# A decoder kernel: in both cross-attentions Pool subtracts the maximum, the scores are transposed, then the exponential leaves PSUM

## The chip, the cores and the metric

The kernel runs on one core of one Trainium2 chip. The metric is device time in microseconds (us) of one execution. The core has five engines, which run their own instruction streams in order and wait for each other by semaphores: TensorE (PE in the profile; PEld is its weight load), VectorE (DVE), ScalarE (ACT), GpSimd (POOL) and SyncE (SP), which here issues every DMA. SBUF holds 128 partitions of working memory; matrix products land in PSUM, of which the kernel uses eight banks of 128 x 512 float32.

## The reference

Two decoder layers over x of shape (8, 256, 256): eight batches, 256 tokens, width 256, all float32. Every sublayer is followed by a residual sum and a layer norm (post-norm):

```
x = LN(x + gated_recurrence(x))                       # layer 0
x = LN(x + cross_attention(x, ctx, bias, mask))       # 16 heads of 16
x = LN(x + ternary_ffn(x))                            # needs max|x| over ALL batches
x = LN(x + self_attention(x))                         # layer 1, relative positions
x = LN(x + cross_attention(x, ctx, mask))
x = LN(x + gated_ffn(x))                              # hidden 768
```

The attention that matters here is, for a head h,

```
scores = (q_h @ k_h.T) / 4 + bias       # 256 x 256; masked keys get -inf
attn   = softmax(scores, axis=keys)
out_h  = attn @ v_h                     # 256 x 16
```

There are 8 x 16 heads in each of three attentions: 128 in the first cross-attention, 128 in the self-attention, 128 in the second cross-attention.

## The kernel before

**An order worked out in advance.** The kernel doesn't loop over stages. Every batch of every sublayer is a Python generator that yields operations (`do(engine, cost, ready, emit)`), DMAs, buffer requests (`get`) and events. A planner (`Order.run`) keeps a clock for each engine, takes the operation that can start first, settles near-ties by an urgency number, and emits its instructions. Costs are written in by hand. The result is a fixed instruction stream for each engine, so what the chip does late the later instructions of that engine wait for. `place(x, n)` gives urgencies: the items stand in a row, the eight first cross-attentions at 0 to 7, then self-attentions and second cross-attentions interleaved by `S1_AT` and `X1_AT`, then feed-forwards by `F1_AT`. `loads()` has urgency 0, so all weight loads come before the first context load in SP's queue. Filler tasks (`keys_values`: the second cross-attention's keys and values, kept in DRAM) take what is left.

**Stages.** Recurrences of all batches come first, then the eight first cross-attentions with the last recurrences between them. A barrier follows (the ternary feed-forward needs the largest value of all batches), then the ternary feed-forward, then self-attention. Self-attention sends its relative-position scores and its probabilities through DRAM scratch (`sk`, `pb`), to shift each row by its position. From the third self-attention on, second cross-attentions run between; when all self-attentions are done, gated feed-forwards join.

**An attention item** (`ai` 0, 1, 2 for first cross, self, second cross; `it.whole` is true for the two cross-attentions) projects q, k and v, then goes through four quads n = 0 to 3, each of four heads j. `quad` (L897) computes the scores of four heads into four PSUM banks (`s`, L914). For each head DVE then adds bias or mask, negates, writes the result to SBUF (`sn`, one of four `s_bufs`) and finds the row's minimum `nm`, that is minus the maximum (L942, two instructions of 128x256, each followed by an accumulator read). `head` (L952) lets ACT take exp(nm - sn) into a slice of `p` (a tile of four heads; three of them), with the row sum as accumulator (L958, two instructions and two accumulator reads). PE transposes the head's 256 x 256 in four 128 x 128 pieces into PSUM (`pt`, L503), and ACT or DVE, whichever the planner finds earlier, copies it to SBUF (`pts`, L291/L292; eight buffers). `values` (L983) multiplies by v: head j of a quad lands in partitions 32j to 32j+31 of the item's PV bank. The two heads i = 0, 1 that share these partitions are told apart by v, which is 32 columns wide with zeros beside the 16 values, so both add into one result.

`scales` (L1019) turns the sums into reciprocals on DVE (`rsum`), POOL spreads them over 256 columns (`rsw`, L1028), PE transposes them (`ps_rs`), a copy brings them to `oT`. `attend_out` (L1041) multiplies PV by `oT` on DVE (L1050), projects (`pso`, L520), adds the residual (`xb`, L1058 on POOL, L1070 on DVE) and normalises. At most two items hold a PV bank at a time (`pv_left`).

**Buffers that are shared.** `p` (3), `s` (4), `v` (2), `q` (3), `k` (2) and `y` (2) serve all three attentions. The query and key weights arrive padded (32 columns a head of which 16 are used, 512 KB a matrix, `wpad`) in a `p` tile, and POOL compacts them (`compact`, L477).

## Time and profile before

Three runs took 817.53, 820.76 and 822.42 us; the median is 820.76.

| what | value |
|---|---|
| median of the runs | 820.76 us |
| span of the profiled execution (first to last instruction) | 807.4 us |
| the profiled execution's own time | not listed; the three runs stand 10.1, 13.4 and 15.0 us above this span |
| instructions | 21273 |
| DMA | 77.67 MB, mean 96 GB/s, 177681 packets, 155046 of them under 512 B |
| granted PE clock, mean | 0.998 |

In the page's groups a line is: source line, engine, operation, output <- input tiles, shape, count | busy us, mean ns of one | idle time of the engine just before, and what ended it. A busy share is an average over stages with different limits, so the stretches are read one by one. Matmuls are pipelined: a record of one includes its latency, and a busy PE is not a PE at its peak. A float32 matmul leaves two records, a transpose one. The profile lists the busy time of weight loads separately from matmuls because the two overlap.

### The profile page before, as it was taken

Reading aid. Unit: us, or ns where it says so; the run is one execution under the profiler, and the core shown is the slowest. Engines: PE = TensorE matmul, PEld = TensorE weight load, DVE = VectorE, ACT = ScalarE, POOL = GpSimd, SP = SyncE. Lnnn points to the kernel's source line nnn. Section 1 sums busy time; section 2 is a strip of 40 time slices with the busy share of each in tenths; the row PEclk is TensorE's granted clock in tenths of the full one; section 3 lists DMA queues with packets and bytes.
Section 4 is the critical chain, followed back from the end, with each engine's and each line's share of the span. In section 5 each row is a group of like instructions: output and inputs, shape, how many; then the busy total and the mean of one; then the engine's idle time right before and its main releaser. Section 6 shows DMA issues by size and latency. Waiting matters only on the chain. (4 is left out here: it accounts for less than half of the span.)

```text
span 807.4 us, 21273 instructions
## 1 busy us (share of the span) xinstructions
PE 774.9 (96%) x7175; PEld 597.3 (74%) x7175; DVE 703.4 (87%) x2461; ACT 629.7 (78%) x2036; POOL 210.4 (26%) x398
## 2 busy tenths in 40 slices
PE   7999999999999999997999999999999999999995
PEld 6787777777766787665767677767776767899885
DVE  3998989989787698887799999898898999989986
ACT  2339999899988457786597799999999899845942
POOL 4440321122111044233333304313242323110010
PEclk9999999999999999999999999999999999999999
DMA  5736352100100449889978706743656333100001
GB/s 183 221 120 97 26 74 50 40 15 28 40 14 15 144 116 220 173 166 154 192 159 170 137 7 145 166 87 89 121 120 139 85 72 114 40 15 16 26 14 39
DMA packets 177681, 77.67 MB, mean 96 GB/s; under 512 B 155046, under 2 KB 171430, under 8 KB 177574
## 3 DMA queue, kind: packets, MB, share of 16 engines
q1 hardware_dynamic: 177574, 76.32, 43.4%
q8 instruction: 57, 0.93, 0.5%
q14 instruction: 50, 0.41, 0.2%
HBM read 41.66 MB, written 34.64 MB: 94 GB/s over the span
## 5 line engine op out<-in xcount | busy, mean ns | idle before, releaser
L958 ACT ACTIVATE p<-sn,nm 128x256 f32<-128x256 f32 x768 | 381.5, 510 | 14.1 <-DVE nm L942 8.2
L503 PE MATMUL pt<-ident,p 128*128 128x128 f32 x1536 | 208.4, 278 | 4.3 <-ACT p L958 1.8
L503 PEld LDWEIGHTS pt<-ident,p 128*128 128x128 f32 x1536 | 169.4, 141 | 50.5 <-ACT p L958 30.2
L292 ACT COPY pts<-pt 128x512 f32<-128x512 f32 x277 | 148.3, 591 | 34.5 <-PE pt L503 29.6
L958 ACT ACTIVATION_READ_ACCUMULATOR p<-sn,nm 128x1 f32 x768 | 154.4, 201 | 0.0
L914 PE MATMUL s<-k,q 32*128 32x256 f32 (+2 forms) x1792 | 118.6, 370 | 0.5 <-ACT pts L292 0.3
L998 PE MATMUL pv<-pts,v 128*32 128x256 f32 x1536 | 104.0, 385 | 0.0
L942 DVE CUSTOM_DVE_ANT_0 sn<-s,bias 128x256 f32<-128x256 f32 x256 | 93.1, 419 | 10.0 <-ACT p L958 5.8
L942 DVE CUSTOM_DVE_ANT_0 sn<-s,hide 128x256 f32<-128x256 f32 x256 | 92.8, 418 | 8.2 <-PE s L914 5.3
L942 DVE CUSTOM_DVE_ANT_0 sn<-s,band 128x256 f32<-128x256 f32 x256 | 92.3, 418 | 8.6 <-PE s L914 3.5
L914 PEld LDWEIGHTS s<-k,q 32*128 32x128 f32 x1792 | 77.2, 185 | 30.1 <-issue 20.1
L291 DVE COPY pts<-pt 128x512 f32<-128x512 f32 x107 | 71.1, 683 | 6.7 <-PE pt L503 6.3
L998 PEld LDWEIGHTS pv<-pts,v 128*32 128x32 f32 x1536 | 41.7, 109 | 41.5 <-issue 19.1
L942 DVE DVE_READ_ACCUMULATOR2_ANT nm<- 128x1 f32 x768 | 63.0, 82 | 0.0
L1028 POOL COPY rsw<-rsum 128x512 f32<-128x512 f32 x24 | 14.6, 610 | 157.4 <-DVE rsum L1022 139.0
L520 PE MATMUL pso<-wvo,oT 128*128 128x256 f32 x192 | 46.3, 385 | 0.4 <-ACT pts L292 0.4
L520 PEld LDWEIGHTS pso<-wvo,oT 128*128 128x128 f32 x192 | 35.1, 190 | 7.8 <-issue 1.3
L1354 POOL COPY band<-ends 64x256 f32<-64x256 f32 x64 | 21.5, 360 | 70.8 <-DVE nm L942 70.8
L1426 DVE TENSOR_REDUCE acc<-tail 128x8 f32<-128x864 f32 x32 | 33.4, 1045 | 5.3 <-POOL tail L1415 5.3
L1327 POOL COPY w<-w 128x504 f32<-128x504 f32 x32 | 19.6, 613 | 68.8 <-DVE w L291 40.7
L1709 ACT ACTIVATE sg<-fg 128x512 f32<-128x512 f32 x24 | 14.3, 599 | 21.7 <-PE fg L1698 21.6
L520 PE MATMUL psv<-wvo,ctxT 128*128 128x256 f32 x128 | 30.8, 384 | 0.0
(197 smaller groups left out, 1321.3 us busy)
## 6 DMA issues: line engine op xcount, KB each, us to landing
sk<-w SPq DMA_DIRECT2D x32, 416.0 KB
band<-sk SPq DMA_DIRECT2D x64, 104.0 KB
pb<-p SPq DMA_DIRECT2D x64, 104.0 KB
band<-sk SPq DMA_DIRECT2D x64, 84.0 KB
pb<-p SPq DMA_DIRECT2D x64, 84.0 KB
acc<-pb SPq DMA_DIRECT2D x32, 156.0 KB
ctxT<-in_ctxT SPq DMA_DIRECT2D x16, 256.0 KB
wpad<-in_qk_w SPq DMA_DIRECT2D x6, 512.0 KB
```

The lines of the kernel that those rows point to most:

```text
L291: ("DVE", on_dve(n), lambda: nc.vector.tensor_copy(dst, src)),
L292: ("ACT", on_act(n), lambda: nc.scalar.copy(dst, src)),
L503: nc.tensor.transpose(ps[:, c, t * P : (t + 1) * P], src[:, t, c * P : (c + 1) * P], ident)
L520: nc.tensor.matmul(ps[:, t, :], srcT[:, c, t * P : (t + 1) * P], w[:, c, :], start=(c == 0), stop=(c == KC - 1),)
L914: nc.tensor.matmul(ps[j].tile[:, t, first : first + w], it.q.tile[32 * j : 32 * j + 32, c, t * P : (t + 1) * P], k[32 * j : 32 * j + 32, c ...
L942: nc.vector.tensor_tensor_reduce(out=s.tile[:, t, :], in0=ps[j].tile[:, t, :], in1=tile[:, t, :], scale=-1.0, scalar=3e38, op0=ALU.add, op ...
L958: nc.scalar.activation(p.tile[:, j, q, :], s.tile[:, q, :], AF.Exp, bias=nm[:, q : q + 1], scale=-1.0, accum_out=it.sum_of(q, h),)
L998: nc.tensor.matmul(it.pv.tile[32 * j : 32 * j + 32, c, :], it.v.tile[:, k, head_of(n, j), :], pts.tile[:, k, :], start=(k == 0 and i == 0 ...
L1028: lambda: nc.gpsimd.tensor_copy(wide.tile.rearrange("p t (h d) -> p t h d", d=DH), rs.unsqueeze(3).to_broadcast([P, NQ, H, DH]),),
L1327: nc.gpsimd.tensor_copy(w.tile[:, :, NR:], w.tile[:, :, NR - 1 : NR].to_broadcast([P, HH, PBW - NR]))
L1354: nc.gpsimd.tensor_copy(band.tile[0:BLK, :, t, lo:hi], it.ends[c][0:BLK, t, i:HH:2].unsqueeze(2).to_broadcast([BLK, 4, hi - lo]),)
L1426: lambda: nc.vector.tensor_reduce(acc[:, c, :, own, 1], tail.tile, AX.X, ALU.add),
```

## The change

In the two cross-attentions (`whole`), the work of a head is reordered:

- DVE writes negated scores and their row minimum as before. POOL then subtracts the minimum in place (two instructions of 128x256). PE transposes the scores, not the probabilities. ACT takes the exponential while moving the result from PSUM to `pts`, in one instruction of 128x512, without accumulators. No choice between ACT and DVE is left at this point.
- The row sums come from the value product. v is still 32 columns wide, but the 16 columns beside the values hold ones, so a head's 32 partitions of PV hold 16 values and 16 copies of the sum. Heads i = 0 and 1 can no longer add into one result. The quads are taken in the order (c, i) = (0,0), (1,0), (0,1), (1,1); after two quads DVE transposes the PV bank in 32x32 blocks to an SBUF tile `u`, and the next two quads start the bank anew. The third value product therefore waits for that transpose. `divided` then takes reciprocals of the sums, multiplies, and after the second half transposes back into `oT`. `scales` and the multiplication in `attend_out` remain for self-attention alone.
- Scores of the first cross-attention lie in twelve slices of the three `p` tiles, those of the second in the four `s` tiles. Self-attention writes its scores straight into `p` and takes the exponential in place.
- `v` is split: two tiles with ones (the second cross-attention uses one of them), and two zeroed tiles for self-attention. `y` and `u` have two tiles in layer 0 and one in layer 1.
- The transposes ask for their bank and their `pts` tile together, for all three attentions; the planner learns to treat operations that need two kinds of buffers, and to drop its reservations (`patient`) when it would otherwise be stuck.
- Query and key weights are loaded without padding, in two DMAs a matrix of 128 KB each, in runs of 64 bytes; `compact` is gone.
- The first cross-attention's mask is loaded into the tile that holds its float form; the second one's float mask becomes bfloat16.

The diff, cut to its core and moved left by one step:

```diff
-            if needs:
-                slots = needs[0].slots
-                if id(slots) in kept:
-                    continue
-                if len(slots.idle) < len(needs):
-                    if ready <= self.clock + 0.5:
+            short = False
+            for slots in {id(x.slots): x.slots for x in needs}.values():
+                count = sum(x.slots is slots for x in needs)
+                if id(slots) in kept or len(slots.idle) < count:
+                    short = True
+                    if patient and ready <= self.clock + 0.5:
                         kept.add(id(slots))
...
                 slots.idle.sort()
-                ready = max(ready, slots.idle[len(needs) - 1][0])
+                ready = max(ready, slots.idle[count - 1][0])
+            if short:
+                continue
             for engine, cost, emit in ways:
...
 pv_left = Slots(2, None)
-p_bufs = slots(work, "p", 3, [P, 4, NQ, S])
+ps_tiles = [work.tile([P, 4, NQ, S], F32, name=f"p{i}") for i in range(3)]
+p_bufs = kept(ps_tiles)
+early_bufs = kept([t[:, j] for t in ps_tiles for j in range(4)])
 pts_bufs = slots(work, "pts", 8, [P, NQ, S])
-s_bufs = slots(work, "s", 4, [P, NQ, S])
+late_bufs = slots(work, "s", 4, [P, NQ, S])
+u_tiles = [work.tile([P, NB, 3, DH], F32, name="u0"), w0.tile([P, NB, 3, DH], F32, name="u1")]
 q_bufs = slots(work, "q", 3, [P, KC, S])
...
 oT_bufs = slots(work, "oT", 2, [P, KC, S])
-y_bufs = slots(work, "y", 2, [P, NQ, D])
+y_tiles = [work.tile([P, NQ, D], F32, name="y0"), w0.tile([P, NQ, D], F32, name="y1")]
 xb_bufs = slots(work, "xb", 2, [P, NQ, D])
...
-v32s = []
-for i in range(2):
-    t = const.tile([P, NQ, H, 32], F32, name=f"v32_{i}")
-    nc.gpsimd.memset(t, 0.0)
-    v32s.append(t)
-v_bufs = kept(v32s)
+v_tiles = [pool.tile([P, NQ, H, 32], F32, name=f"v{i}") for i, pool in enumerate((const, w0))]
+for t in v_tiles:
+    nc.gpsimd.memset(t, 1.0)
+class Layer:
+    def __init__(self, n, s_bufs):
+        self.s_bufs = s_bufs
+        self.y_bufs, self.u_bufs, self.v_bufs = (kept(x[:n]) for x in (y_tiles, u_tiles, v_tiles))
+layers = [Layer(2, early_bufs), Layer(1, late_bufs)]
...
                 )
-            packed = yield from get(p_bufs, f"wpad{o}")
-            t = packed.tile.rearrange("p k c s -> p (k c s)")[:, 0 : KC * H * 32]
-            t = t.rearrange("p (c o) -> p c o", c=KC)
-            w = pool.tile([P, KC, D], F32, tag=f"wqk{o}", name=f"wqk{o}")
-            ready = yield from dma(
-                [packed.at], 524288,
-                lambda: nc.sync.dma_start(
-                    out=t, in_=chunked(qk_w[o])
-                ),
-            )
-            order.spawn(50 + o, compact(o, packed, t, w, ready))
+            w = wqk[o] = pool.tile([P, KC, D], F32, tag=f"wqk{o}", name=f"wqk{o}")
+            for c in range(KC):
+                events["wqk", o] = yield from dma(
+                    [0.0], 131072,
+                    lambda: nc.sync.dma_start(
+                        out=w[:, c, :].rearrange("p (h d) -> p h d", d=DH),
+                        in_=qk_w[o][c * P : (c + 1) * P, :].rearrange(
+                            "p (h w) -> p h w", w=32
+                        )[:, :, 0:DH],
+                    ),
+                    60,
+                )
             wvo[o] = pool.tile([P, KC, D], F32, tag=f"wvo{o}", name=f"wvo{o}")
...
         return (what, self.ai, self.b, *more)
+def parts_of(it, n):
+    if it.whole:
+        return n % 2, n // 2
+    return n // 2, n % 2
+def value_columns(it, v):
+    if it.whole:
+        return v.rearrange("p (h w) -> p h w", w=32)[:, :, 0:DH]
+    return bass.AP(
+        tensor=v.tensor, offset=v.offset, ap=[list(v.ap[0]), [64, H // 2], [48, 2], [1, DH]],
+    )
...
         order.spawn(urgency(it, n + 1, -12), quad(it, n + 1, parts, bias))
-    p = yield from get(p_bufs, f"p{it.name}_{n}", t_s)
+    p = None
+    if not it.whole:
+        p = yield from get(p_bufs, f"p{it.name}_{n}", t_s)
     left = [4]
...
     for j in range(4):
-        s = yield from get(s_bufs, f"sn{it.name}_{n}_{j}", t_s)
+        if it.whole:
+            s = yield from get(it.layer.s_bufs, f"sn{it.name}_{n}_{j}", t_s)
+            dst, t_dst = s.tile, s.at
+        else:
+            dst, t_dst = p.tile[:, j], p.at
         nm = small.tile([P, NQ], F32, tag="nm", name=f"nm{it.name}_{n}_{j}")
...
                 nc.vector.tensor_tensor_reduce(
-                    out=s.tile[:, t, :], in0=ps[j].tile[:, t, :], in1=tile[:, t, :], scale=-1.0,
+                    out=dst[:, t, :], in0=ps[j].tile[:, t, :], in1=tile[:, t, :], scale=-1.0,
                     scalar=3e38, op0=ALU.add, op1=ALU.min, accum_out=nm[:, t : t + 1],
                 )
-        t = yield from do("DVE", 0.7, [t_s, t_b, t_bias, s.at], emit)
+        t = yield from do("DVE", 0.7, [t_s, t_b, t_bias, t_dst], emit)
         ps[j].drop(t)
-        order.spawn(urgency(it, n), head(it, n, j, p, s, nm, t, left, times))
+        if it.whole:
+            order.spawn(urgency(it, n), head_whole(it, n, j, s, nm, t))
+        else:
+            order.spawn(urgency(it, n), head(it, n, j, p, nm, t, left, times))
     if it.ai == 1:
         it.bands[n].drop(t)
-def head(it, n, j, p, s, nm, t, left, times):
-    h = head_of(n, j)
+def head_whole(it, n, j, s, nm, t):
+    def emit():
+        for q in range(NQ):
+            nc.gpsimd.tensor_scalar(
+                s.tile[:, q, :], s.tile[:, q, :], nm[:, q : q + 1], None, ALU.subtract
+            )
+    t = yield from do("POOL", 0.66, [t], emit)
+    ps = Held(banks, f"pt{it.name}_{n}_{j}")
+    pts = Held(pts_bufs, f"pts{it.name}_{n}_{j}")
+    t = yield from do("PE", TURNS, [t, ps, pts], lambda: transposed(ps.tile, s.tile))
+    s.drop(t)
+    t = yield from do(
+        "ACT", on_act(512), [t, pts.at],
+        lambda: nc.scalar.activation(pts.tile, ps.tile, AF.Exp, scale=-1.0),
+    )
+    ps.drop(t)
+    it.turned[n].append((j, pts, t))
+    if len(it.turned[n]) == 4:
+        order.spawn(urgency(it, n), values(it, n))
+def head(it, n, j, p, nm, t, left, times):
+    h = head_of(*parts_of(it, n), j)
     def emit():
...
             nc.scalar.activation(
-                p.tile[:, j, q, :], s.tile[:, q, :], AF.Exp, bias=nm[:, q : q + 1], scale=-1.0,
+                p.tile[:, j, q, :], p.tile[:, j, q, :], AF.Exp, bias=nm[:, q : q + 1], scale=-1.0,
                 accum_out=it.sum_of(q, h),
             )
-    t_e = yield from do("ACT", 1.0, [t, p.at], emit)
-    s.drop(t_e)
+    t_e = yield from do("ACT", 1.0, [t], emit)
     it.t_sums.append(t_e)
...
     times.append(t_e)
-    if it.ai == 1 and len(times) == 4:
+    if len(times) == 4:
         it.tails(n, p, left, max(times))
     ps = Held(banks, f"pt{it.name}_{n}_{j}")
-    t = yield from do("PE", TURNS, [t_e, ps], lambda: transposed(ps.tile, p.tile[:, j]))
+    pts = Held(pts_bufs, f"pts{it.name}_{n}_{j}")
+    t = yield from do("PE", TURNS, [t_e, ps, pts], lambda: transposed(ps.tile, p.tile[:, j]))
     left[0] -= 1
...
         p.drop(t)
-    pts = yield from get(pts_bufs, f"pts{it.name}_{n}_{j}", t)
     t = yield from copy([t, pts.at], pts.tile, ps.tile)
...
 def values(it, n):
-    c, i = divmod(n, 2)
+    c, i = parts_of(it, n)
     t_v = yield from event(it.key("v"))
...
         it.pv = Held(banks, f"pv{it.name}")
+    if it.whole and n == 2:
+        t_turned = yield from event(it.key("turned", 0))
+        t_v = max(t_v, t_turned)
     parts = sorted(it.turned[n], key=lambda x: x[0])
...
                     it.pv.tile[32 * j : 32 * j + 32, c, :],
-                    it.v.tile[:, k, head_of(n, j), :],
+                    it.v.tile[:, k, head_of(c, i, j), :],
                     pts.tile[:, k, :],
-                    start=(k == 0 and i == 0 and (it.whole or c == 0)),
-                    stop=(k == NQ - 1 and i == 1 and it.whole),
+                    start=(k == 0 and (it.whole or n == 0)),
+                    stop=(k == NQ - 1 and it.whole),
                     tile_position=(0, 32 * j),
...
         it.v.drop(t)
+    if it.whole and n % 2 == 1:
+        order.spawn(urgency(it, n), divided(it, n // 2, t))
+    elif n == NS - 1:
         order.spawn(urgency(it, NS), attend_out(it, t))
     events[it.key("values", n)] = t
+def divided(it, i, t):
+    if i == 0:
+        it.u = yield from get(it.layer.u_bufs, f"u{it.name}", t)
+        it.rec = small.tile([P, 2, NB], F32, tag="rec", bufs=4, name=f"rec{it.name}")
+    u = it.u.tile
+    t = yield from do(
+        "DVE", on_dve(512), [t, it.u.at],
+        lambda: nc.vector.transpose(
+            u[:, :, i : i + 2, :].rearrange("p n a d -> p n (a d)"),
+            it.pv.tile.rearrange("p c (n e) -> p (c n) e", e=32),
+        ),
+    )
+    events[it.key("turned", i)] = t
+    if i == 1:
+        it.pv.drop(t)
+        it.token.drop(t)
+    def emit():
+        nc.vector.reciprocal(it.rec[:, i, :], u[:, :, i + 1, 0])
+        nc.vector.tensor_tensor(
+            u[:, :, i, :], u[:, :, i, :],
+            it.rec[:, i, :].unsqueeze(2).to_broadcast([P, NB, DH]), ALU.mult,
+        )
+    t = yield from do("DVE", 0.6, [t], emit)
+    if i == 0:
+        return
+    it.oT = yield from get(oT_bufs, f"oT{it.name}", t)
+    t = yield from do(
+        "DVE", on_dve(512), [t, it.oT.at],
+        lambda: nc.vector.transpose(
+            it.oT.tile.rearrange("p c (n e) -> p (c n) e", e=32),
+            u[:, :, 0:2, :].rearrange("p n a d -> p n (a d)"),
+        ),
+    )
+    it.u.drop(t)
+    order.spawn(urgency(it, NS), attend_out(it, t))
...
     ai, b = it.ai, it.b
-    t = yield from event(it.key("scales"))
+    t = t_pv
+    if ai == 1:
+        t = yield from event(it.key("scales"))
+        t_pv = yield from event(it.key("distances"))
+        t = yield from do(
+            "DVE", on_dve(512), [t, t_pv],
+            lambda: nc.vector.tensor_tensor(it.oT.tile, it.pv.tile, it.oT.tile, ALU.mult),
+        )
+        it.pv.drop(t)
+        it.token.drop(t)
     oT = it.oT
-    if ai == 1:
-        t_pv = yield from event(it.key("distances"))
-    t = yield from do(
-        "DVE", on_dve(512), [t, t_pv],
-        lambda: nc.vector.tensor_tensor(oT.tile, it.pv.tile, oT.tile, ALU.mult),
-    )
-    it.pv.drop(t)
-    it.token.drop(t)
     xb = yield from get(xb_bufs, f"xb{it.name}", t)
...
     t_b = yield from dma([bias.at], 262144, lambda: nc.sync.dma_start(out=bias.tile, in_=tokens(bias_in[b])))
-    mask = yield from get(mask_bufs, f"mask{b}")
-    t_m = yield from dma([mask.at], 262144, lambda: nc.sync.dma_start(out=mask.tile, in_=tokens(mask0_in[b])))
+    neg = yield from get(neg_bufs, f"neg{b}")
+    mask = neg.tile.bitcast(I32)
+    t_m = yield from dma([neg.at], 262144, lambda: nc.sync.dma_start(out=mask, in_=tokens(mask0_in[b])))
     yield from project_k(
...
     )
-    neg = yield from get(neg_bufs, f"neg{b}", t_m)
-    t = yield from do(
-        "DVE", on_dve(512), [t_m, neg.at],
-        lambda: nc.vector.tensor_scalar(
-            neg.tile, mask.tile, 0.0, NEG_INF, ALU.is_equal, ALU.mult
-        ),
-    )
-    mask.drop(t)
+    t = yield from do(
+        "DVE", on_dve(512), [t_m],
+        lambda: nc.vector.tensor_scalar(neg.tile, mask, 0.0, NEG_INF, ALU.is_equal, ALU.mult),
+    )
     t_b = yield from do(
...
-hide_bufs = slots(work, "hide", 2, [P, NQ, S])
+hide_bufs = slots(work, "hide", 2, [P, NQ, S], BF16)
...
```

## The prediction

> **What bounds the kernel now.** I read the busy totals first, then the busy times by stage, then the groups by line and shape, the chain that ended last, single tiles, and the DMA share microsecond by microsecond.
>
> ```profile
> PE 774.9 (96%) x7175; PEld 597.3 (74%) x7175; DVE 703.4 (87%) x2461; ACT 629.7 (78%) x2036; POOL 210.4 (26%) x398
> ```
> ```profile
> 0.00:57.00 57.00, 50.95 (x248) 43.99 (x252) 41.90 (x97) 16.01 (x35) 24.48 (x44) 1.00 0.57 181
> 57.00:262.00 205.00, 202.14 (x1875) 149.64 (x1868) 179.33 (x717) 187.96 (x639) 37.42 (x52) 1.00 0.22 41
> 330.00:430.00 100.00, 93.41 (x960) 66.26 (x962) 85.19 (x285) 76.66 (x260) 35.62 (x78) 1.00 0.90 164
> 430.00:700.00 270.00, 265.91 (x2831) 195.87 (x2824) 248.64 (x956) 248.99 (x856) 79.33 (x149) 1.00 0.49 108
> 700.00:807.40 107.40, 97.77 (x863) 89.31 (x862) 91.00 (x232) 59.86 (x154) 12.62 (x24) 0.99 0.06 21
> ```
> The columns are the stretch, then PE, PEld, DVE, ACT, POOL busy (instructions), clock, DMA share, GB/s. The stretches are: recurrences; first cross-attention; self-attention alone (DMA share 0.90); self- and second cross-attention together; the feed-forward with the last cross-attentions. In the two attention stretches ACT is busy 92% and DVE 87 to 92%.
>
> PE's 96% overstates it, because pipelined matmuls are shown with their latency. The chain shows what PE needs when it never waits:
>
> ```profile
> 702.24 2.62 PE pt L503 x24
> 534.37 1.86 PE pv L998 x32
> 549.05 1.12 PE s L914 x24
> 552.09 1.73 PE psq L509 x8
> 715.32 5.76 PE psd L1740 x48
> ```
> That is 109 ns a transpose, 216 ns a full matmul record, 58 ns a value record, 70 ns for 256 score columns, and by the psd pieces 120 ns a feed-forward record. Multiplied by the counts in the groups, PE needs 712 us of the 807.4. By stage it needs 184.8 of 205, 82.9 of 100, 245.5 of 270 and 94.5 of 107.4. So PE is the real bound, and a faster ACT can win at most PE's stall: 20 us in the first cross-attention, 24.5 us in the mixed stretch.
>
> ```profile
> L958 ACT ACTIVATE p<-sn,nm 128x256 f32<-128x256 f32 x768 | 381.5, 510 | 14.1 <-DVE nm L942 8.2
> L292 ACT COPY pts<-pt 128x512 f32<-128x512 f32 x277 | 148.3, 591 | 34.5 <-PE pt L503 29.6
> L958 ACT ACTIVATION_READ_ACCUMULATOR p<-sn,nm 128x1 f32 x768 | 154.4, 201 | 0.0
> L291 DVE COPY pts<-pt 128x512 f32<-128x512 f32 x107 | 71.1, 683 | 6.7 <-PE pt L503 6.3
> L1028 POOL COPY rsw<-rsum 128x512 f32<-128x512 f32 x24 | 14.6, 610 | 157.4 <-DVE rsum L1022 139.0
> L1354 POOL COPY band<-ends 64x256 f32<-64x256 f32 x32 | 12.5, 391 | 70.8 <-DVE nm L942 70.8
> ```
> The reader should see ACT's three costs per head here, a share of the copies falling to DVE, and POOL mostly idle.
>
> **The change, part by part.**
>
> *ACT, 256 of the 384 heads.* The exponentials and their accumulator reads go. In the timeline eight exponentials with reads take 3.92 us from start to start, 0.98 us a head, 251 us in all. The copy out of PSUM becomes an exponential out of PSUM, which I price like the 128x512 copy (591 ns; the Tanh from PSUM, sg<-fg, shows 599). In the first cross-attention ACT falls from 188 to about 78 us of 205 (minus 125.6 for exponentials, 50.7 and 1.8 for copies, plus 128 x 0.534). None of that is time by itself; it removes ACT as the engine that stalls PE (pt waited 9.3 and 13.0 us for L958 in the two stretches).
>
> *POOL.* Per head two subtractions of 128x256. Bounds: half of the 617 ns that a 128x512 tensor_scalar takes (0.31), and half of the two-input 1.27 us (0.64). Nearest is L1354: 391 ns alone, four in 1.28 us. I take 0.34 each, 0.68 a head, 174 us in all. Less rsw for 16 items (9.8) and six compactions (4.5), POOL goes from 210 to 370 us; in the first cross-attention from 37 to 120 of 205. POOL's queue also holds the bias sums, residual sums and norm roots (up to 1.27 us each), and all three now queue with the heads. A burst of four heads takes 2.7 us on POOL and 2.8 us on DVE (0.345 us an L942 start to start), so POOL keeps pace: cost nothing, hidden behind DVE. Without that cover it is the second rival.
>
> The row behind this is one-input POOL work at 617 ns for 512 elements. The Trainium skill (GPSIMD Engine Reference, Engine selection) speaks against the change: elementwise work belongs on VectorE, GPSIMD being about twice slower with two inputs, though roughly line-rate with one. By its two-input warning, twice the time, the sum would be the second rival's; by its one-input remark it stays.
>
> *DVE.* Removed in the first cross-attention: 33 copies (21.8 us), oT multiplies (5.5), reciprocals (2.8), scale copies (3.4). Added per item: three transposes, two reciprocals, two multiplies. No 32x32 transpose is in the trace; its bounds are the 0.42 us of a 128x256 operation and twice a 128x512 PSUM copy (1.37); I take the copy's 0.68, the nearest in bytes. Reciprocals 0.35 (L1022), multiplies 0.42 (128x256 L885): 3.58 us an item, 28.6 for eight. DVE goes from 179 to 174 us.
>
> DVE operations with two SBUF inputs, or in the fast mode, collide with POOL:
>
> ```profile
> L684 POOL TENSOR_SCALAR a<-z x8: 617/618/1657, 9.1 to 80.8; 128x512 f32<-128x512 f32 x8
> L554 DVE TENSOR_SCALAR xn<-xb,mv_l0x,rs_l0x x16: 401/408/1358, 93.7 to 270.7; 128x256 f32<-128x256 f32 x16
> L942 DVE CUSTOM_DVE_ANT_0 sn<-s,bias x256: 361/419/426, 57.8 to 254.5; 128x256 f32<-128x256 f32 x128
> ```
> Some wait out a whole operation (1.36 against 0.41 us), but L942, which reads PSUM, never does (426 at most). About 60 such DVE operations fall into the stage, each waiting 0 to 0.35 us; a third of that is 7 us, giving DVE 181. The price of these waits lies inside the stage estimates below.
>
> *PE.* The scale transposes leave for 16 items (4 x 0.109 each): 7 us, all on the path. Added: the third value quad waits until DVE has turned the first half out of the PV bank; behind it in PE's queue stand the next scores and transposes. The order puts other work there; uncovered it is a 0.68 us transpose plus DVE's queue, about 1 us x 16.
>
> *Buffers.* Self-attention writes scores straight into p and loses the four staging tiles, but no longer shares p or v with cross-attention; the second cross-attention has one v, one u. Transposes now also need a free pts tile, of which eight exist. A mask load now waits for POOL's bias sum (1.27 us) too, one item ahead of its use. Two memsets of v (0.95 us each) join POOL where it idles 12 us at the layer's start. Counted at 0, covered by the other item in flight; minus 3 to plus 5.
>
> *Loads.* Six padded loads of 512 KB plus compaction become twelve loads of 128 KB in 64-byte runs, 2048 packets each. All stand in SP's queue before the first context load (issued at 34.28 us). Nearest row: two acc<-pb gathers, 2048 packets of 156 bytes.
>
> ```profile
> 648.00:649.00 1.00, 1.00 (x17) 0.42 (x16) 1.00 (x5) 1.00 (x5) 0.00 (x0) 1.00 0.40 67
> 649.00:650.00 1.00, 1.00 (x12) 0.92 (x9) 1.00 (x6) 1.00 (x5) 0.00 (x0) 1.00 1.19 201
> 650.00:651.00 1.00, 0.88 (x9) 0.48 (x10) 1.00 (x9) 1.00 (x4) 0.00 (x0) 1.00 0.48 65
> ```
> Shares add to 2.07 us of 16 engines: 16 ns a packet, 2.07 us a load. The upper bound is the sk<-zero writes, 252 bytes at 101 GB/s: 40 ns, 5.1 us a load. Eight such loads stand where three padded ones (1.36 us each at the 387 GB/s seen near 38 us) stood before the context: 16.5 minus 4.1, so 12 us later. Meanwhile PE and DVE do the recurrences that used to run beside the start (about 2.7 x 6 us of PE work). What is lost is the ramp that they covered: plus 5 us, between 0 and 12; at 40 ns plus 30.
>
> The row gives 16 ns. The Trainium skill (DMA: Bandwidth & Descriptors, Specifications) wants at least 512 bytes a transfer for line rate. An estimate from that page, each run charged as 512 bytes at 387 GB/s, is 21 ns: context 17 us later and the sum 5 us worse.
>
> *The sum by stages.* First cross-attention: PE needs 181.3; at the present density (0.902) 201 (minus 4), at 0.97 as around 60 to 100 us 187 (minus 18). With DVE still near 90% I take 0.925: 196, minus 9. Mixed stretch: PE 242.4; minus 3 at 0.909, minus 20 at 0.97; ACT falls from 249 to about 160 and DVE to about 232, so 0.94: minus 12. Self-attention alone is held by its DMAs: 0. Feed-forward: minus 1 (minus 3 to plus 4; the item's new end, about 1.3 us longer after the last value matmul, against a last quad some 3 us shorter). Start: plus 5. Total minus 17: span 790. The profiled execution's own time is not given; the three runs stand 10 to 15 us above its span, the median 13.4. So 804 us.
>
> **The rivals.**
> *Denser than forecast.* Both mixed stretches at 0.97, start free: minus 18, 20 and 1, so span 768, 782 us. For: 60 to 100 us ran so dense. Against: DVE near 90%.
> *Loads make it slower (other side).* At 40 ns a packet the start costs 30 instead of 5: span 815, 829 us. It decides at about 33 ns, where 17 us more is lost. For: 64 bytes are shorter than any large transfer here. Against: 156-byte reads took 16.
> *POOL becomes the bound.* At 0.64 us a subtraction POOL needs 196 us in the first stage, above PE's 181: that stage turns to plus 3, the mixed stretch to minus 4: span 810, 824 us. For: never run here with a per-partition operand. Against: L684 and L1354.
> *Gain given back on DVE.* Transposes at twice the copy's time add 16 us, collisions at full 0.35 us 14 more: DVE 204, first stage 0, mixed minus 8: span 803, 817 us.
>
> **How the numbers follow.** Three runs spread by 0.6%, so half a per cent, 4.1 us, is about what can be told from no change. Chances: forecast 0.46, denser 0.15, loads 0.12, POOL 0.12, DVE 0.11, other slowdowns 0.04. Faster 0.46 + 0.15 + 0.03 of DVE = 0.64; same 0.08 + 0.02 of POOL = 0.10; slower 0.26. The likeliest case alone spans 792 to 816. The range leaves out half of the denser case's tail and the far slow ones: 778 to 832.
>
> **What would show it.** Right: ACT near 430 us, PE's records 64 fewer, POOL near 370 with subtractions near 0.34 us, first scores some 7 us later than 56.6, the two attention stretches shorter. Wrong: transposes waiting for POOL, value matmuls waiting for DVE's transposes, PE idle before 70 us, or DVE the engine always full.

## The result: slower by 22%, with POOL's pass at 0.92 us

The changed kernel takes 1001.3 us (median; 1000.65 to 1007.22) against 820.08 us: a ratio of 1.2215, 95% interval 1.2162 to 1.2269. The forecast was 804 us, in a range of 778 to 832. The profiled execution's span went from 807.4 to 999.3 us. The busy totals after:

```profile
PE 857.7 (86%) x7111; PEld 615.6 (62%) x7111; DVE 672.1 (67%) x2397; ACT 462.1 (46%) x1146; POOL 666.6 (67%) x888
```
ACT fell as meant (629.7 to 462.1 us), PE has the 64 records fewer that were forecast, DVE fell too. But POOL rose from 210.4 to 666.6 us, not to 370. The groups by shape say why (busy us, mean ns of one, idle time before it and what ended that):

```profile
L982 POOL TENSOR_SCALAR sn<-sn,nm 128x256 f32<-128x256 f32 x256 | 236.2, 940 | 49.4 <-DVE nm L964 49.3
L993 ACT ACTIVATE pts<-pt 128x512 f32<-128x512 f32 x256 | 146.8, 598 | 247.0 <-PE pt L510 246.3
L982 POOL TENSOR_SCALAR p<-p,nm 128x256 f32<-128x256 f32 x256 | 232.6, 927 | 10.7 <-DVE nm L964 10.7
L510 PE MATMUL pt<-ident,p 128*128 128x128 f32 x1024 | 164.9, 292 | 41.3 <-POOL p L982 33.8 <-DVE nm L964 3.9 <-ACT p L1005 1.9
L510 PEld LDWEIGHTS pt<-ident,p 128*128 128x128 f32 x1024 | 118.5, 146 | 96.4 <-POOL p L982 59.2 <-ACT p L1005 13.4 <-issue 13.2
```
The two rows of L982 sum to 469 us where 174 were forecast. PE's transpositions now wait for them, and ACT's exponential waits 246 us for PE: the slow link is two steps ahead of ACT. Busy times by stage, in the columns of the stages shown of before (the second row is the first cross-attention, the fourth self- and second cross-attention together):

```profile
0.00:68.00 68.00, 60.25 (x284) 48.07 (x288) 48.56 (x115) 18.73 (x41) 24.81 (x44) 1.00 0.63 125
68.00:330.00 262.00, 214.28 (x1713) 142.43 (x1706) 150.80 (x659) 93.52 (x177) 248.13 (x278) 0.94 0.17 32
404.00:515.00 111.00, 102.38 (x994) 73.34 (x994) 87.24 (x309) 84.13 (x282) 37.88 (x87) 0.97 0.93 164
515.00:860.00 345.00, 300.64 (x2789) 202.53 (x2788) 233.31 (x908) 184.28 (x503) 252.39 (x341) 0.93 0.45 90
860.00:999.30 139.30, 118.01 (x976) 101.34 (x976) 104.52 (x288) 50.15 (x88) 73.24 (x87) 0.96 0.05 16
```
In the first cross-attention POOL is busy 248.1 of 262 us, 95%. POOL's timeline there (start, us, instructions) has hardly a gap:

```profile
132.02 21.98 POOL L982 TENSOR_SCALAR p<-p,nm 128x256 f32<-128x256 f32 x24 [2.45 <-DVE nm L964]
153.98 1.27 POOL L1150 TENSOR_TENSOR xb<-x_l0a,rows 128x512 f32<-128x512 f32 x1
155.20 1.27 POOL L1239 TENSOR_TENSOR bias<-bias,neg 128x512 f32<-128x512 f32 x1
```
24 subtractions in 21.98 us are 0.916 us each. The residual and bias sums stand in the same queue. The shares of the chain that ended last, by engine, where POOL has nearly as much as PE:

```profile
PE 32%; POOL 30%; DVE 20%; DMA 5%; issue 5%; SPq 4%; ACT 3%; POOLq 0%; DVEq 0%; ACTq 0%
```

For all comparisons below I cut each profiled span at three places, read from the first and last start of DVE's pass over the scores (p or sn <- s with bias, band, hide): the first scores, the end of the first cross-attention's scores, the first scores of self-attention, the end. Times in us:

| kernel | to first scores | first cross-attention | to first self scores | from there to the end | span |
|---|---|---|---|---|---|
| before | 57.8 | 196.7 | 55.0 | 497.9 | 807.4 |
| changed | 68.5 | 261.2 | 74.1 | 595.5 | 999.3 |
| e2, no subtraction | 68.4 | 182.9 | 61.3 | 510.0 | 822.6 |
| e8, multiply and add | 67.5 | 189.9 | 57.4 | 514.5 | 829.3 |
| e5, before + loads | 68.7 | 192.4 | 55.3 | 503.5 | 819.9 |
| e12, before + reserved copy tile | 57.2 | 196.5 | 54.9 | 521.2 | 829.8 |
| e13, before + scores into p | 58.5 | 193.2 | 53.3 | 516.7 | 821.7 |
| e14, e8 + padded loads | 45.2 | 212.7 | 57.9 | 512.4 | 828.2 |
| e17, first cross alone | 42.7 | 212.9 | 58.0 | 520.2 | 833.8 |

Each row is a single profiled execution. The row "before" is a quick one: beside e5 and the later runs the spans of the kernel before lay between 811.9 and 818.9 us, so a difference of less than some 10 us from that row says little. The runs stand on several chips, with medians of the kernel before between 811.2 and 820.1 us. So whole times are compared by their ratio to the kernel before on the same chip; the loss to explain is 22.15%, 181 us.

### The profile page after: what moved, and what is told of

Its sections match the earlier page's. It is cut to its first block, busy times and chain, and to the rows that moved or that the text cites. A ratio compares the mean times of both kernels' runs of the same rounds, so it can differ in the third digit from the quotient of the medians.

```text
span 999.3 us, 20913 instructions
## 1 busy us (share of the span) xinstructions
PE 857.7 (86%) x7111; PEld 615.6 (62%) x7111; DVE 672.1 (67%) x2397; ACT 462.1 (46%) x1146; POOL 666.6 (67%) x888
## 4 chain that ended last, share of the span: by engine, by line
PE 32%; POOL 30%; DVE 20%; DMA 5%; issue 5%; SPq 4%; ACT 3%; POOLq 0%; DVEq 0%; ACTq 0%
POOL sn L982 16%; POOL p L982 9%; PE pt L510 7%; PE s L930 6%; DVE p L964 5%; PE pv L1047 5%; DMA sk<-w 3%; PE psq L516 2%; PE psv L527 2%; PE pso L527 2%; PE psk L516 2%; DVE sn L964 1%; SPq L438 1%; POOL xb L1150 1%; ACT p L1005 1%
## 5 line engine op out<-in xcount | busy, mean ns | idle before, releaser
L982 POOL TENSOR_SCALAR sn<-sn,nm 128x256 f32<-128x256 f32 x256 | 236.2, 940 | 49.4 <-DVE nm L964 49.3
L993 ACT ACTIVATE pts<-pt 128x512 f32<-128x512 f32 x256 | 146.8, 598 | 247.0 <-PE pt L510 246.3
L982 POOL TENSOR_SCALAR p<-p,nm 128x256 f32<-128x256 f32 x256 | 232.6, 927 | 10.7 <-DVE nm L964 10.7
L510 PEld LDWEIGHTS pt<-ident,p 128*128 128x128 f32 x1024 | 118.5, 146 | 96.4 <-POOL p L982 59.2
L964 DVE CUSTOM_DVE_ANT_0 p<-s,bias 128x256 f32<-128x256 f32 x256 | 92.0, 416 | 59.3 <-PE s L930 53.9
L1005 ACT ACTIVATE p<-p,nm 128x256 f32<-128x256 f32 x256 | 127.0, 504 | 10.2 <-DVE nm L964 8.9
L510 PE MATMUL pt<-ident,sn 128*128 128x128 f32 x512 | 93.9, 303 | 38.7 <-POOL sn L982 35.7
L964 DVE CUSTOM_DVE_ANT_0 p<-s,band 128x256 f32<-128x256 f32 x256 | 92.3, 417 | 26.5 <-PE s L930 17.6
L510 PEld LDWEIGHTS pt<-ident,sn 128*128 128x128 f32 x512 | 61.0, 149 | 73.1 <-POOL sn L982 63.5
L303 ACT COPY pts<-pt 128x512 f32<-128x512 f32 x95 | 52.1, 587 | 18.3 <-PE pt L510 17.9
```

Of the source, the lines that this page charges most:

```text
L303: ("ACT", on_act(n), lambda: nc.scalar.copy(dst, src)),
L510: nc.tensor.transpose(ps[:, c, t * P : (t + 1) * P], src[:, t, c * P : (c + 1) * P], ident)
L964: nc.vector.tensor_tensor_reduce(out=dst[:, t, :], in0=ps[j].tile[:, t, :], in1=tile[:, t, :], scale=-1.0, scalar=3e38, op0=ALU.add, op1=A ...
L982: nc.gpsimd.tensor_scalar(s.tile[:, q, :], s.tile[:, q, :], nm[:, q : q + 1], None, ALU.subtract)
L993: lambda: nc.scalar.activation(pts.tile, ps.tile, AF.Exp, scale=-1.0),
L1005: nc.scalar.activation(p.tile[:, j, q, :], p.tile[:, j, q, :], AF.Exp, bias=nm[:, q : q + 1], scale=-1.0, accum_out=it.sum_of(q, h),)
```

## The experiments

The theory (A): POOL's pass costs 0.92 us where 0.34 was forecast; that makes POOL the bound, and that is the loss. Rivals: any POOL pass here is slow, because DVE holds the way to SBUF (B); another part of the change costs (C); the written order with its price of 0.66 us for a pair costs (D).

### e1: a constant in place of the maximum

```diff
-  s.tile[:, q, :], s.tile[:, q, :], nm[:, q : q + 1], None, ALU.subtract
+  s.tile[:, q, :], s.tile[:, q, :], 0.0, None, ALU.subtract
```


> POOL subtracts the constant 0 in place of the head's maximum, so the maximum is left out of the softmax; instructions, shapes and order are those of the changed kernel. Theory A (the price of the subtraction with one operand per partition, 0.92 us for 128x256, is the loss, because POOL becomes the bound): with a constant it costs what L684's row gives, 0.31 to 0.35 us; POOL falls from 667 to about 370 us, PE again sets the time, 790 to 815 us. Rival B (any POOL pass over SBUF data of this shape costs 0.9 us, because DVE holds the port): duration and time stay, 0.9 us and above 980 us. Rival C (what costs is something else of the change: loads, the value quad's wait, the order): subtractions get shorter, the time stays above 900 us.

949.7 us, ratio 1.173 (1.169 to 1.176). By tile (ns min/median/max) the subtraction still stands at 0.85 us:

```profile
L982 POOL TENSOR_SCALAR sn<-sn x256: 837/848/1367, 488.7 to 905.4; 128x256 f32<-128x256 f32 x128
```
So the operand per partition was not the price: it adds 0.07 us. Theory A's number for this run was wrong. B's duration came near (0.9 us expected), its time (above 980 us) did not. C's figures, a shorter pass and still above 900 us, came out, so e1 alone decides nothing between them.

### e2: no subtraction

```diff
-                nc.gpsimd.tensor_scalar(
-                    s.tile[:, q, :], s.tile[:, q, :], nm[:, q : q + 1], None, ALU.subtract
-                )
+                pass
```


> The subtraction is left out (and so is the maximum), the order written out is that of the changed kernel to the instruction. It shows what the rest of the change is worth with a free POOL. Theory A: POOL near 200 us, 785 to 805 us. Rival C: above 900 us. A middle case would be 820 to 850 us: the rest of the change alone is then slower than the kernel before, which the forecast's minus 17 us excludes.

823.9 us, ratio 1.016 (1.013 to 1.019): the middle case. With the same written order and POOL at 199.9 us, the loss is 1.6%, not 22.15%: some 168 of the 181 us hang on the pass. The first cross-attention is 14 us shorter than before the change, but in this pair of traces everything else takes more. The rest of the change is no gain.

### e3: a dearer pair in the order

```diff
-        t = yield from do("POOL", 0.66, [t], emit)
+        t = yield from do("POOL", 1.4, [t], emit)
```


> The changed kernel with the pair of subtractions entered at 1.4 us in the order's cost table, not 0.66, so that other work is put beside it. Theory A: an item of the first cross-attention still has 32 pairs... 29 us of subtractions and 4 us of other POOL work, so that stage stays near 270 us, and the time between 970 and 1010 us. Rival D (the loss comes from an order made with a wrong price, POOL's other work and the values standing behind the heads): below 930 us.

961.7 us (one time), a ratio of 1.186. The first cross-attention's scores span 240.9 us, not 261.2 and not the 270 that I expected. Neither bound is met: the order's wrong price makes 3.6 of the 22 points, some 30 us of the loss, as I read it by keeping PE from other work while POOL is full; the larger part stays, since the passes are as slow as before. (An item has 16 pairs, not the 32 of the expectation; 29 us is right for 32 passes.)

### e4: exponential on ACT before the transposition, sums from the ones

```diff
-                nc.gpsimd.tensor_scalar(
-                    s.tile[:, q, :], s.tile[:, q, :], nm[:, q : q + 1], None, ALU.subtract
+                nc.scalar.activation(
+                    s.tile[:, q, :], s.tile[:, q, :], AF.Exp, bias=nm[:, q : q + 1], scale=-1.0,
...
-        t = yield from do("POOL", 0.66, [t], emit)
+        t = yield from do("ACT", 0.6, [t], emit)
...
-            lambda: nc.scalar.activation(pts.tile, ps.tile, AF.Exp, scale=-1.0),
+        t = yield from copy([t, pts.at], pts.tile, ps.tile)
```


> One part undone: ACT takes the exponential from SBUF with the maximum as its bias, as before the change, but without summing; transposition, copy out of PSUM by ACT or DVE, sums from the ones, divided after the transposes as in the change. Nothing is left out. Theory A: POOL near 200 us; the accumulator reads of 256 heads (512 by 0.2 us) are gone, ACT near 530 us; PE sets the time, 795 to 815 us. Rival C: above 900 us.

849.8 us, ratio 1.049 (1.046 to 1.052), outside both expectations. ACT is at 621.6 us. Its timeline shows six exponentials without the read:

```profile
162.32 2.52 ACT L982 ACTIVATE p<-p,nm 128x256 f32<-128x256 f32 x6
```
That is 0.42 us each, against 0.49 with the read (eight in 3.92 us before). The accumulator reads were worth 0.07 us each and not the 0.2 that their rows show. So ACT is relieved by moving the exponential, hardly by dropping the sums. Why e4 is 26 us slower than e2, whose ACT is at 450.8 us, was not separated: ACT's load and the pair's price of 0.6 us in the order (two passes take 0.84) both differ.

### e6, e7 and e9: what makes the pass slow

Three runs change the operations or the size of the pass, each with one form in the first cross-attention (`it.ai == 0`) and another in the second. First e6, which also drops the sign from the exponential:

```diff
+                if it.ai == 0:
+                    nc.gpsimd.tensor_scalar(
+                        s.tile[:, q, :], s.tile[:, q, :], -1.0, nm[:, q : q + 1], ALU.mult, ALU.add
+                    )
+                else:
+                    nc.gpsimd.tensor_scalar(
+                        s.tile[:, q, :], s.tile[:, q, :], -1.0, 0.0, ALU.mult, ALU.add
+                    )
```


> What makes the POOL pass cost 0.92 us where L688 of the kernel before passes twice as many elements, in place and in the same type, in 0.617 us? Here the first cross-attention multiplies by -1 and adds the maximum (one operand per partition, the exponential then without the sign), the second one multiplies by -1 and adds the constant 0, so there the maximum is left out; shape and place are those of the changed kernel. If the operation counts (multiply and add with both constants as in L688 is fast, a lone subtraction is not): 0.31 to 0.40 us in the second one; if the operand per partition counts as well, 0.4 to 0.9 us in the first. If neither counts, but the slice of 256 in a wider tile or the in-place pass: 0.85 to 0.92 us in both, and the time stays at 940 to 1000 us.

Then e7, one pass a head:

```diff
+            if it.ai == 0:
+                nc.gpsimd.tensor_scalar(s.tile, s.tile, 0.0, None, ALU.subtract)
+            else:
+                nc.gpsimd.tensor_tensor(
+                    s.tile, s.tile, nm.unsqueeze(2).to_broadcast([P, NQ, S]), ALU.subtract
+                )
```


> One size changed: one pass of 128x512 a head instead of two of 128x256. In the first cross-attention it subtracts the constant 0 (the maximum is left out there), in the second one it subtracts the maxima spread over the columns, as a two-input operation. If the pass has a large fixed part (at the 128x256 pass's 0.85 us with a constant): 0.9 to 1.1 us a head in the first one, which would then be near 200 us long; if it is paid by the element: 1.6 to 1.7 us, and the first stage stays near 240 us. For the two-input form the two-input POOL operations of the trace (1.27 us for 128x512) say 1.2 to 1.4 us, which is cheaper than the two passes with an operand per partition (1.83 us).

And e9:

```diff
+                if it.ai == 0:
+                    nc.gpsimd.tensor_scalar(
+                        s.tile[:, q, :], s.tile[:, q, :], nm[:, q : q + 1], 1.0, ALU.subtract, ALU.mult
+                    )
+                else:
+                    nc.gpsimd.tensor_scalar(
+                        s.tile[:, q, :], s.tile[:, q, :], 0.0, None, ALU.add
+                    )
```


> Is it the subtraction that is slow on POOL, or any lone operation without a second one? First cross-attention: subtract the maximum and then multiply by 1 (two operations, a subtraction among them, nothing left out). Second one: add the constant 0 alone (the maximum is left out there). If the subtraction is slow: 0.9 us or more in the first, about 0.41 us in the second. If the lone operation is slow: about 0.49 us in the first, 0.85 us in the second. If both matter: 0.9 and 0.85 us; if only multiply first is fast, the same two figures, and the run doesn't tell these apart.

They took 832.0, 897.3 and 1029.1 us (one time each). The passes by tile, of e6, e7 and e9:

```profile
L983 POOL TENSOR_SCALAR p<-p,nm x256: 477/487/729, 69.3 to 258.2; 128x256 f32<-128x256 f32 x128
L987 POOL TENSOR_SCALAR sn<-sn x256: 399/408/854, 428.0 to 788.2; 128x256 f32<-128x256 f32 x128
```
```profile
L982 POOL TENSOR_SCALAR p<-p x128: 1478/1489/1623, 68.8 to 301.0; 128x512 f32<-128x512 f32 x128
L984 POOL TENSOR_TENSOR sn<-sn,nm x128: 1031/1039/1512, 473.2 to 854.4; 128x512 f32<-128x512 f32 x128
```
```profile
L983 POOL TENSOR_SCALAR p<-p,nm x256: 1132/1142/1304, 68.8 to 396.8; 128x256 f32<-128x256 f32 x128
L987 POOL TENSOR_SCALAR sn<-sn x256: 837/848/1363, 566.8 to 985.9; 128x256 f32<-128x256 f32 x128
```
All carry the name TENSOR_SCALAR but for the two-input one, all are in place, in the same tiles, beside the same DVE work, so B falls. What counts is which operations the pass performs; why, no run shows. Multiply then add: 0.408 us with constants, 0.487 with an operand per partition. A lone add or subtract of a constant: 0.848 both. A lone subtract with an operand per partition: 0.92. Subtract, then multiply, with an operand per partition: 1.142. These are medians of single records; from start to start the order is the same (24 passes with a lone constant in 19.71 us of e1, eight of multiply and add with constants in 3.00 us of e6). Of e9's cases the last two are nearest, which it can't tell apart, though 1.142 is 0.24 us above both: of the forms tried only multiply-then-add is fast. By the element: from 256 to 512 columns the lone operation grows by 0.641 us, 2.5 ns a column; multiply and add grows from 0.408 to the 0.617 us of L688 of before (another tile and stage), 0.8 ns a column. Even the two-input form, 1.04 us a head, is cheaper than two lone subtractions (1.83); the forecast's ceiling came from the dearer two-input row of 1.27 us.

The Trainium skill (GPSIMD Engine Reference, Engine selection) calls one-input work on this engine roughly line-rate. Multiply and add is near that: 0.408 us with constants and 0.487 with an operand per partition, where DVE's 128x256 TENSOR_SCALAR between SBUF tiles took 0.408 (L554 of before, two operands per partition). The lone operation is not: 0.848 us, twice that.

### e8: multiply and add everywhere

```diff
-  s.tile[:, q, :], s.tile[:, q, :], nm[:, q : q + 1], None, ALU.subtract
+  s.tile[:, q, :], s.tile[:, q, :], -1.0, nm[:, q : q + 1], ALU.mult, ALU.add
...
-        t = yield from do("POOL", 0.66, [t], emit)
+        t = yield from do("POOL", 0.95, [t], emit)
...
-            lambda: nc.scalar.activation(pts.tile, ps.tile, AF.Exp, scale=-1.0),
+            lambda: nc.scalar.activation(pts.tile, ps.tile, AF.Exp),
```


> The changed kernel with one edit: POOL multiplies the negated scores by -1 and adds the maximum (0.487 us in the run before) where it subtracted (0.92 us); the exponential then goes without the sign, and the order's price of the pair is 0.95 us. Nothing is left out. Theory A (POOL's price is the whole large loss): POOL near 200 + 512 x 0.47 = 440 us, no longer full in the first cross-attention (60 of 182 us of PE's need), first cross-attention 183 to 192 us long, time 820 to 836 us, between the run without a subtraction and the mixed run. Rival: POOL's in-order queue, not its sum, delays the heads: above 845 us.

833.6 us, ratio 1.0215 (1.018 to 1.025), as expected. Its busy totals, and its first cross-attention and mixed stretch:

```profile
PE 783.0 (94%) x7111; PEld 596.7 (72%) x7111; DVE 674.7 (81%) x2404; ACT 444.2 (54%) x1132; POOL 444.5 (54%) x887
```
```profile
67.00:258.00 191.00, 190.16 (x1772) 142.15 (x1764) 160.96 (x673) 88.20 (x176) 150.32 (x292) 1.00 0.22 44
...
424.00:700.00 276.00, 264.49 (x2788) 192.23 (x2783) 230.06 (x911) 177.66 (x499) 169.24 (x343) 1.00 0.57 113
```
PE is busy all of the first cross-attention again. The ratio falls from 1.2215 to 1.0215: of 181 us the choice of operation makes about 164, with nothing left out of the computation. The price of 0.95 in the order, which e8 also changes, is not what did it: e6 kept 0.66 and took 832.0 us (ratio 1.019). The other 17 us (2.1%) are the rest of the change, which was forecast to win 17; by e2 (1.6%, with no pass at all) POOL has little part in them.

### e5, e10 and e14: the loads

e5 puts the twelve loads into the kernel before; e10 moves eight of them behind the first context loads in e8; e14 puts the padded loads and the compaction back into e8.

```diff
-                packed = yield from get(p_bufs, f"wpad{o}")
...
-                order.spawn(50 + o, compact(o, packed, t, w, ready))
+                w = wqk[o] = pool.tile([P, KC, D], F32, tag=f"wqk{o}", name=f"wqk{o}")
+                for c in range(KC):
+                    events["wqk", o] = yield from dma(
...
```


> The kernel before with one part of the change alone: twelve loads of 128 KB in 64-byte runs straight into wqk, no padded loads and no compaction on POOL. The forecast priced this part at plus 5 us (0 to 12, plus 30 if a packet costs 40 ns). In the changed kernel's trace the first scores come 10.7 us later than in the kernel before, and the run without the subtraction still ends 15 us of span later than the kernel before. If the loads are that loss: plus 10 to plus 15 us, first scores near 68 us. If the recurrences fill the wait: plus 0 to plus 5 us, and the rest of the loss comes from the order and the buffers of the attention stages.

```diff
-        for a in range(3):
+        yield from layer_loads(0)
+        order.spawn(115, later_loads())
...
```


> The run with multiply and add, and the weight loads of the two later attentions (eight of the twelve loads in 64-byte runs) put behind the first two items' context loads in SP's queue. If those loads delay the start (alone they cost the kernel before 6.5 us): first scores 8 to 12 us earlier, near 58 us, time 4 to 8 us below the run with multiply and add alone. If the recurrences fill that wait: 0 to 2 us.

```diff
-                w = wqk[o] = pool.tile([P, KC, D], F32, tag=f"wqk{o}", name=f"wqk{o}")
...
+                packed = yield from get(pad_bufs, f"wpad{o}")
...
+                order.spawn(50 + o, compact(o, packed, t, w, ready))
```


> The run with multiply and add, and the padded loads with POOL's compaction put back (staged in the third p tile). If the loads in 64-byte runs cost here what they cost the kernel before alone: minus 4 to minus 9 us against the run with multiply and add, 824 to 830 us. If the context's wait is covered here: minus 2 to plus 2 us.

Alone: 823.0 us, ratio 1.0078 (1.005 to 1.011), 6.4 us; first scores at 68.7 us. SP's timeline of e5 shows it held by issuing them (start, us for two); four pairs take 14.2 us ahead of the first context load:

```profile
32.20 5.09 SPq L397 DMA_DIRECT2D wqk<-in_qk_w  x2
...
39.17 2.72 SPq L397 DMA_DIRECT2D wqk<-in_qk_w  x2
...
43.82 2.93 SPq L397 DMA_DIRECT2D wqk<-in_qk_w  x2
...
48.49 3.46 SPq L397 DMA_DIRECT2D wqk<-in_qk_w  x2
...
53.86 0.43 SPq L1135 DMA_DIRECT2D ctxT<-in_ctxT  x1
```
In the kernel before a padded load (`wpad`) holds SP for 0.5 us, and the first context load is issued at 34.28 us.

But within the change they cost nothing: e10 took 832.0 us, e14 835.0 us, e8 833.6 us, with overlapping intervals. In e10 and e14 the first scores come at 43 to 45 us, 22 to 25 us earlier, and the first cross-attention ends where it did (256.3 and 257.9 against 257.4 us). PE did the recurrences early or late, and their sum stayed: at the forecast's prices e14's first cross-attention, 212.7 us long, holds 192 us of PE's need, that of e8 172.

### e11: the change in the first cross-attention alone

e11 is e10 with the second cross-attention put back.

```diff
-            self.whole = ai != 1
+            self.whole = ai == 0
...
-    late_bufs = slots(work, "s", 4, [P, NQ, S])
+    late_bufs = None
```


> The run with the later loads, and the second cross-attention put back: exponential and sums on ACT from SBUF, scales turned on PE, zero-padded values, heads in the old order, no staging tiles (its scores go straight into the p tiles, of which there are four). So the change is made in the first cross-attention alone. Theory E (the mixed stretch is where the rest of the change loses): the mixed stretch goes back to the density of the kernel before, 0.91 and not 0.87, time 795 to 812 us, below the kernel before. Rival F (the loss lies in what both share now, self-attention's scores written into p and its transposes taking a copy tile): no better than the run with the later loads, 815 to 830 us.

832.1 us, ratio 1.019 (1.017 to 1.021): as F said no better than e10 (832.0), and not E's number. Put back in e10's order, the second cross-attention's old path is neither gain nor loss, though ACT's load is 98 us higher. The busy totals of e10 and then of e11:

```profile
PE 781.3 (94%) x7111; PEld 595.1 (72%) x7111; DVE 676.6 (81%) x2405; ACT 445.2 (54%) x1135; POOL 442.4 (53%) x887
```
```profile
PE 783.4 (94%) x7143; PEld 599.5 (72%) x7143; DVE 688.3 (83%) x2425; ACT 543.4 (65%) x1600; POOL 327.6 (39%) x641
```

### e12, e13 and e15: what is left

e12: the reserved copy tile and the changed search, in the kernel before. e13: scores straight into p, in the kernel before, with a fourth p tile in place of the staging tiles. e15: three staging tiles in e8.

```diff
-        t = yield from do("PE", TURNS, [t_e, ps], lambda: transposed(ps.tile, p.tile[:, j]))
+        pts = Held(pts_bufs, f"pts{it.name}_{n}_{j}")
+        t = yield from do("PE", TURNS, [t_e, ps, pts], lambda: transposed(ps.tile, p.tile[:, j]))
...
-        pts = yield from get(pts_bufs, f"pts{it.name}_{n}_{j}", t)
```


> The kernel before with two parts of the change alone, both of which only shape the written order: a transposition is put into the order only when a copy tile is free as well, and the changed search for the next instruction. If these are the loss of the rest: plus 6 to plus 12 us. If not: minus 2 to plus 2 us.

```diff
-    p_bufs = slots(work, "p", 3, [P, 4, NQ, S])
+    p_bufs = slots(work, "p", 4, [P, 4, NQ, S])
...
-                        out=s.tile[:, t, :], in0=ps[j].tile[:, t, :], in1=tile[:, t, :], scale=-1.0,
+                        out=p.tile[:, j, t, :], in0=ps[j].tile[:, t, :], in1=tile[:, t, :], scale=-1.0,
```


> The kernel before with one part of the change alone, for all three attentions: DVE writes the scores straight into the p tile, ACT takes the exponential in place, the four staging tiles are gone and their memory makes a fourth p tile. If the in-place pass or the missing staging costs: plus 5 to plus 12 us. If not: minus 3 to plus 2 us.

```diff
-    late_bufs = slots(work, "s", 4, [P, NQ, S])
+    late_bufs = slots(work, "s", 3, [P, NQ, S])
```


> The run with multiply and add, and one size changed: three staging tiles for the second cross-attention in place of four (two hundred and fifty-six passes go through them). If that count holds the mixed stretch: plus 8 to plus 25 us. If it does not: below plus 4 us.

e12: 832.3 us, ratio 1.020 (1.017 to 1.023), all of it after the first self scores. The changed search alone writes the order of before, instruction for instruction, so it is the reservation: a rule of the order that adds no work. e13: 823.3 us, 1.008 (1.006 to 1.011). e15: 864.7 us, 1.060 (1.056 to 1.065), 31 us above e8: as I read it the mixed stretch hangs on how many heads of the second cross-attention may be under way. Whether a fifth tile would help was not tried.

### e16, e17 and e18: without the reservation

e16 is e8, where only the second cross-attention keeps the reservation; e17 is e11 with none, and e18 is e17 with the padded loads in their old place. The edit in self-attention's path:

```diff
-        pts = Held(pts_bufs, f"pts{it.name}_{n}_{j}")
-        t = yield from do("PE", TURNS, [t_e, ps, pts], lambda: transposed(ps.tile, p.tile[:, j]))
+        t = yield from do("PE", TURNS, [t_e, ps], lambda: transposed(ps.tile, p.tile[:, j]))
...
+        pts = yield from get(pts_bufs, f"pts{it.name}_{n}_{j}", t)
```


> The run with multiply and add, but in the first cross-attention and in self-attention the copy tile is taken after the transposition, as in the kernel before; only the second cross-attention still reserves it (the order can't be completed otherwise). If the reservation is the loss here as it is in the kernel before (plus 16 us): 817 to 826 us. If it is the second cross-attention's own reservation and its four staging tiles: 829 to 835 us, no change.

> The run that makes the change in the first cross-attention alone (832 us), now with no copy tile reserved anywhere. If the reservation is its loss: 808 to 820 us; the first cross-attention itself saves 7 us or so, and straight writing into p costs up to 7. If not: 828 to 834 us.

> The run before this one with the padded loads and the compaction put back in their old place, so that of the change only the first cross-attention's path (multiply and add on POOL, exponential out of PSUM, sums from the ones) and the straight writing into p are left. If the loads cost as they do alone: 3 to 8 us less than that run, 802 to 814 us, at or below the kernel before. If they are covered: within 2 us of it.

833.8, 834.5 and 839.7 us; ratios 1.021 (1.019 to 1.024), 1.022 (1.020 to 1.025) and 1.029 (1.026 to 1.032). None gives anything back. What costs 16 us in the kernel before is not what holds the changed one, and e17 with the padded loads in their old place is 5 us slower still.

So this part stays open. Of the runs made around e8, all but e15 and e18 lie within 832 and 835 us, whether the loads, the second cross-attention's path or the reservation was undone, and in every one of them most of the excess over the row "before" comes after the first self scores (512 to 520 us against 498; these scores themselves come 4 to 7 us later). Part of that excess is only that row's quick execution. The parts do not add: loads, reservation and straight writing cost 6, 16 and 7 us alone, 29 in sum, and the changed kernel with multiply and add loses 17. A written order that suits the kernel before better than any of its neighbours would look like this; that was argued, not shown. Self-attention's straight writing into p was undone in none of these runs; what it costs beside the rest is not known.

## Why the prediction was wrong, point by point

- **POOL, the step that failed.** "I take 0.34 each, 0.68 a head, 174 us in all ... cost nothing, hidden behind DVE." Measured 0.916 us from start to start, 469 us in all, and not hidden: PE waits for it. Both ends of the range, 0.31 and 0.64, and the value taken came from rows of other operations: L684 multiplies and adds, L1354 copies (on half the partitions), the two-input row adds. The row's name is that of the instruction, and which operations it performs stands only in the code line. For multiply and add the forecast was nearer: 0.408.
- **The rival "POOL becomes the bound" was the right mechanism at too low a price.** Its sum (256 passes at 0.64 us plus some 32 us of other POOL work, 196 us) with 0.916 gives 266 us for the first cross-attention; 261 were measured from its first to its last scores. At its price of 0.64 it ended at 824 us, and the range at 832.
- **Its reading of the mixed stretch failed too.** There POOL is at 252 of 345 us, not full, and the stretch is still far longer: as I read it bursts of heads wait at POOL while it stands idle elsewhere, and the order, made with 0.66 us, puts too little beside them (in e3, made with 1.4 us, the time after the first self scores is 569.6 us, not 595.5).
- **First cross-attention, minus 9: near, but by luck.** In e8 it is 6.8 us shorter, yet not denser. PE's need over the stage's time is 0.900 (171.9 us in 191), against 0.902 before and 0.925 forecast. The stage is shorter because it holds less work, 171.9 us of need where the forecast put 181.3: the first scores come 9.7 us later, and recurrence work that stood inside the stage is done ahead of them. The last scores come at 257.4 us, before at 254.5. ACT is busy 88 of the 191 us, where it was 188 of 205, and PE gained nothing: ACT's load alone did not hold PE there. Without POOL's pass (e2) the density is 0.92 and the last scores come at 251.3 us, so a small gain of the forecast kind may be there when POOL costs nothing.
- **Mixed stretch, minus 12 at density 0.94: failed.** e8 has 0.871 there (240.4 us of PE's need in 276), below the 0.909 of before, with ACT and DVE well under their old load. The step took the two busy engines for the cause of PE's stalls. Relieving both bought nothing here, and giving ACT its load back in e11 cost nothing. The buffers, which the forecast had put at 0 (minus 3 to plus 5), do matter there: one staging tile fewer costs 31 us (e15). What held PE in the kernel before, no run shows.
- **Loads, plus 5 (0 to 12).** Right in size alone (6.4 us), covered within the change. The delay behind it was mis-sized: the first context load is issued 19.6 us later in e5, not 12, and the sum counted what the DMA engines take per packet, not SP's 1.4 to 2.5 us for each issue.
- **From span to time, plus 13.4.** The changed kernel's profiled execution took 1001.0 us with a span of 999.3, 1.7 us more. So the 13.4 us were mostly that the profiled execution of before was quicker than the three timed ones.
- **Small terms.** Transposition on DVE 0.71 us (0.68 forecast), reciprocal 0.25 (0.35), multiply 0.51 on average (0.42); ACT 444 us in e8 (430); records minus 64. The value quad's wait for DVE's transposition is in none of the larger waits.

```profile
PEld pt L510 <- POOL sn L982: 10.9, 26, 1.8
PEld pt L510 <- POOL p L982: 7.5, 18, 0.8
```
These two lines of e8's table of waits (us, times, longest) are what is left of POOL on PE's path; in the changed kernel they are:

```profile
PEld pt L510 <- POOL sn L982: 63.5, 103, 1.3
PEld pt L510 <- POOL p L982: 59.2, 97, 1.0
```
That is the forecast's own sign of being wrong, transpositions waiting for POOL.

## What to carry to other kernels

Price an elementwise pass by a row that performs the same operations, not the same instruction name: on POOL here, multiply-and-add took 0.41 to 0.49 us where a lone add or subtract took 0.85 to 0.92, and writing s - m as -1 * s + m, with the sign taken out of the exponential that follows, gave back about 164 of 181 us. When work moves to an engine, multiply the worst believable price by the count and ask at which price that engine becomes the bound; if the best row is of another operation, the range must reach beyond it. In a kernel whose instruction order is written out in advance, an edit that removes busy time may still lose some 2% through the order and the buffers alone, so a gain that rests on "denser" needs a shown buffer, not a less busy engine.

## What was not expected of the hardware

- POOL's pass over 128x256 fp32 values: 0.408 us (multiply, add; constants), 0.487 (with an operand per partition), 0.848 (lone add or subtract, constant), 0.92 (lone subtract, operand per partition), 1.142 (subtract, multiply; operand per partition).
- ACT's accumulator read is shown with 0.2 us, but leaving it out shortened the exponentials by 0.07 us each (0.49 to 0.42, start to start).
- The granted TensorE clock was lower in the runs in which PE waited more: 0.998 in the kernel before (PE busy 96%), 0.993 in e8 (94%), 0.947 in the changed one (86%), 0.922 in e9 (85%). No run tells what the lower clock cost by itself.
